# Keeping two Winograd partial sums in PSUM banks that ScalarE seeds and TensorE adds to, and holding back three products of a unit instead of two

## The chip, the cores and the metric

The kernel runs on one core of one Trainium2 chip. The metric is the device time of one execution in microseconds (us). Three runs of the kernel before gave 1256.2, 1257.9 and 1260.05 us, so its median is 1257.9 us.

## The reference, cut to what matters

One transformer layer on 2048 tokens of width 512, in fp32: an RWKV block (time mixing and channel mixing) and a gated feed-forward block, each behind a layer norm and added to its input.

```
h, hh = layer_norm(x), layer_norm(x) shifted by one token
k, v, r = three mixes of h and hh, each @ a 512x512 weight
x = x + (sigmoid(r) * wkv(k, v)) @ Wo.T
kk = mix(h, hh) @ Wkey.T            # 512 -> 2048
sr = sigmoid(mix(h, hh) @ Wcr.T)
x = x + sr * (silu(kk) @ Wval.T)    # 2048 -> 512
...
out = (silu(z @ gate.T) * (z @ up.T)) @ down.T      # 512 -> 2 x 2048 -> 512
```

Nearly all of the work is matrix products of 512 tokens with 512x512 blocks of weights.

## The kernel before, in words

**Tiling.** The tokens are worked in four blocks of 512 (`b` = 0 to 3). A product of a 512x512 activation block with a 512x512 weight block is not computed as eight products of 256x256 quarters but as seven, by Winograd's form of Strassen's scheme. One product of quarters is four calls of `nc.tensor.matmul` (two halves `m` of the output by two halves `k` of the contraction), and each call leaves two records in the trace, so a product is eight records of line 527 (4256 such records stand for 532 products). `plain_unit` (L619) does the first eight blocks of weights (k, r, v and out of token blocks 0 and 1) without the scheme; `unit` (L508) does everything else except the last down projection, which `down_product` (L1075) does with two levels of the scheme.

**One unit.** With quarters A of the weights and B of the activations, S and T their prepared sums and differences, the seven products are P1 = A11 B11, P2 = A12 B21, P3 = S4 B22, P4 = A22 T4, P5 = S1 T1, P6 = S2 T2, P7 = S3 T3. Their combination is a chain: with U2 = P1 + P6 and U4 = U2 + P5, the quarters of the result are P1 + P2 at (0, 0), U4 + P3 at (0, 1), U4 + P7 at (1, 1) and, with the signs of the prepared sums, U2 + P7 + P4 at (1, 0). In the code, one PSUM bank `z` collects P1, then P6, then P5, then P7 in place. On the way ScalarE copies it to SBUF three times (`snapshot`, L542 to L544): `s1` after P1, `u2` after P6, `u4` after P5. P2 goes to a bank `v` and P3 to a bank `x` of their own, and VectorE adds them to the copies (`add`, L546; `tt`, L362 and L363). P4 goes onto what `z` holds after P7, and VectorE adds the difference `u2` - `u4` to take the surplus out again. Each finished quarter goes to a `sink(i, j, c)` that the caller gives: two Relus and two exponentials on ScalarE for k (L830 to L841), a Tanh for r and the gate, a Silu for up and the feed-forward gate, VectorE multiplications or additions for v, out, up of the feed-forward and down.

**The order within a unit** is written out by hand: `order = (step1, step2, None, step3, step4, None, step5)` (L604). At each `None` one step held back from the unit before is run (`pop_held`, L502); steps 6 and 7 are appended to `held` for the unit after (L614). So a step that writes `z` again is always two products behind the copy that it has to wait for. A unit over four weight blocks (`down_unit`, L938, one for each token block) takes four products per step, one for each weight block; its order is (step1, step4, step3, step2, step5) (L607), and its step 1 pops held steps between its products (`between`, L539). The last of them (`loose`, token block 3) runs its held steps at once.

**What is mixed in.** Every engine runs its instructions in the order in which this Python program emits them. After every product `tick` (L287) lets background work be emitted: norms, transposes on TensorE (L414), the mixes (`mix`, L455: ScalarE writes `shifted`, L464, VectorE adds `mixed`, L472), sums of operands (`sums_of`, L435), and the preparation of weight sums (`prepare`, L140, whose loads go through GpSimd's queue). The planner counts VectorE time (`cost`, L200) against 88% of 1.72 us per product (`STEP`, `SHARE`) and holds work back when it has run ahead. `later(fn, n)` (L203) puts VectorE work off by n products, `due` (L281) emits it, and `flush` (L209) emits all of it. `Lazy` (L660) forces the operand sums of a unit out when they are first asked for.

**Buffers.** `ps` (L80) is one pool of eight PSUM banks for products and transposes. In the compiled kernel before, banks are handed out again in the order in which they came free. `up` has six SBUF tiles for the copies. The start runs `WARM` = 44 transposes of an identity into a bank (L332 to L334), then the norm, transposes (L769), mixes and the first product of `first_block` (L729).

**The units of the scheme, in order.** gate of block 0; four up units; down of block 0; k, r, v of block 2; gate of block 1; out of block 2; ups, down of block 1; k, r, v of block 3; gate, out, ups, down of block 2; gate, ups, down of block 3; then for each block of the feed-forward four gate and four up units (the first gate unit of the next block is put ahead) and the two-level down product.

Of the kernel before, what the change touches and what calls it, by code (L numbers as in the profile page):

```python
# [9 lines left out]
F32 = mybir.dt.float32  # L10
AF = mybir.ActivationFunctionType
ALU = mybir.AluOpType
# [3 lines left out]
P = 128  # L16
# [4 lines left out]
HB = TB // 2  # L21
# [3 lines left out]
STEP = 1.72  # L25
# [20 lines left out]

A11, A12, A22, A21, S1, S2, S3, S4 = range(8)
B11, B12, B21, B22, T1, T2, T4 = range(7)  # L50
T3 = B12
# [7 lines left out]
def rwkv_ffn_kernel(  # L59
# [8 lines left out]
    nc = tc.nc  # L68
# [8 lines left out]
    opp = ctx.enter_context(tc.tile_pool(name="opp", bufs=3))  # L77
    up = ctx.enter_context(tc.tile_pool(name="up", bufs=6))
    small = ctx.enter_context(tc.tile_pool(name="small", bufs=3))
    ps = ctx.enter_context(tc.tile_pool(name="ps", bufs=8, space=bass.MemoryType.PSUM))  # L80
    dram = ctx.enter_context(tc.tile_pool(name="dram", bufs=1, space=bass.MemoryType.DRAM))


# [8 lines left out]
    def u_tile(name):  # L92
        return up.tile([P, 2, HB], F32, tag="u", name=name)
# [14 lines left out]
    def flat(t):  # L108
        return t.rearrange("p a b -> p (a b)")
# [22 lines left out]
    def raw_quarters(n, eng):  # L132
        raw = []
        for k in range(4):
            t = wring.tile([P, 2, HB], F32, tag="w", name="w")
            eng.dma_start(t, w[n, k])
            raw.append(t)
        return raw
# [61 lines left out]
    def cost(n, fixed=0.135, per=0.00107):  # L200
        spent[0] += max(0.17, fixed + per * n)

    def later(fn, ticks=1):  # L203
        put_off.append([ticks - 1, fn])
# [8 lines left out]
    def step(item, wait):  # L213

        try:
            r = next(item[1])
        except StopIteration:
            item[4].remove(item)
            finished.add(item[2])
            return True  # L220
        return True if wait or r is None else None

    def run_one(wait):


        blocked = False
        for item in list(hot)[:1] + list(background)[:3]:
            ready = item[0]
            if ready is not None and not item[3]:
                if blocked or not ready():  # L230
                    blocked = True
                    continue
                item[3] = True
            if step(item, wait):
                return True
        assert not wait
        return False
# [7 lines left out]
    def prep_one():  # L245
        item = preps[0]
        if item[1] > 0:
            return False
        try:
            if next(item[2]) is not None:  # L250
                item[1] = WAIT
        except StopIteration:
            preps.popleft()
            finished.add(("sums", item[0]))
            if len(preps) > 1 and item[3] > 1:
                begin(preps[1])
            elif preps:
                begin(preps[0])
        return True
# [27 lines left out]
    def tick(length=STEP):  # L287
        for item in preps:
            item[1] -= 1
        slack[0] = max(min(slack[0] + SHARE * length - spent[0], 2.5), -2.5)  # L290
        spent[0] = 0.0
        credit[0] = min(credit[0] + credit[1], 2.0)
        while slack[0] > 0 and (hot or background or preps):
            go = False
            if preps and credit[0] >= 1 and prep_one():
                credit[0] -= 1
                go = True
            elif hot or background:
                go = run_one(False)
            slack[0] -= spent[0]  # L300
            spent[0] = 0.0
            if not go:
                break
# [18 lines left out]
    first = {WK: raw_quarters(WK, nc.sync)}  # L322
    first[WR] = raw_quarters(WR, nc.scalar)
    first[WV] = raw_quarters(WV, nc.sync)
    ident = const.tile([P, P], F32, name="ident")
# [7 lines left out]
    for _ in range(WARM):  # L333
        nc.tensor.transpose(pt[:, 0, 0:P], ident, ident)  # L334

    onem = const.tile([P, 5, NC], F32, name="onem")

    nfirst = const.tile([P, NC], F32, name="nfirst")
# [17 lines left out]
    def size(ap):  # L356
        n = 1
        for d in ap.shape[1:]:
            n *= d
        return n  # L360

    def tt(out, a, b, op):  # L362
        nc.vector.tensor_tensor(out, a, b, op)  # L363
        cost(size(out))
# [131 lines left out]
    held = []  # L496
# [5 lines left out]
    def pop_held():  # L502
        if held:
            length, step = held.pop(0)
            step()
            tick(length)

    def unit(weights, Bs, sink, by_token, done=None, free=None, loose=False):  # L508

        acc, tmp = {}, {}
        last = len(weights) - 1

        def product(z, a, b, first, between=None):
            if first:
                acc[z] = bank()
            pz = acc[z]
            wt = [weight(n, a) for n in weights]
            for g, wg in enumerate(wt):  # L520
                act = Bs[g][b]
                for m in range(2):
                    for k in range(2):
                        lo = slice(m * P, (m + 1) * P)
                        lhsT = act[:, k, lo] if by_token else wg[:, k, lo]
                        rhs = wg[:, k, :] if by_token else act[:, k, :]
                        mm = nc.tensor.matmul(  # L527
                            pz[:, m, :],
                            lhsT=lhsT,
                            rhs=rhs,  # L530
                            start=first and g == 0 and m == 0 and k == 0,
                            stop=g == last and k == 1,
                            skip_group_check=True,
                        )
                latest[:] = [mm.ins.name]
                due()
                if g < last:
                    tick()
                    if between is not None and g > 0:  # L539
                        between()  # L540

        def snapshot(name):  # L542
            tmp[name] = u_tile(name)
            nc.scalar.copy(tmp[name], acc["z"])  # L544

        def add(z, name):  # L546
            tt(tmp[name], acc[z], tmp[name], ALU.add)

        def step1():
            product("z", A11, B11, True, pop_held)  # L550
            snapshot("s1")

        def step2():
            product("v", A12, B21, True)
            add("v", "s1")
            sink(0, 0, tmp["s1"])

        def step3():
            product("z", S2, T2, False)
            snapshot("u2")  # L560

        def step4():
            product("x", S4, B22, True)

        def step5():
            product("z", S1, T1, False)
            snapshot("u4")

            def rest():
                add("x", "u4b")  # L570
                sink(0, 1, tmp["u4b"])

            def both():
                tt(tmp["u2"], tmp["u2"], tmp["u4"], ALU.subtract)
                if loose:
                    tmp["u4c"] = u_tile("u4c")
                    nc.vector.tensor_copy(tmp["u4c"], tmp["u4"])
                    cost(2 * HB)
                tmp["u4b"] = tmp["u4"]
                rest()  # L580

            later(both, 1)

        def step6():
            if loose:
                product("y", S3, T3, True)
                add("y", "u4c")
                sink(1, 1, tmp["u4c"])
                return
            product("z", S3, T3, False)  # L590
            sink(1, 1, acc["z"])

        def step7():
            if loose:
                tt(tmp["u2"], tmp["u2"], tmp["u4c"], ALU.add)
            product("z", A22, T4, loose)
            add("z", "u2")
            sink(1, 0, tmp["u2"])
            if free is not None:
                free()  # L600
            if done is not None:
                later(done, 2)

        order = (step1, step2, None, step3, step4, None, step5)  # L604
        if last > 0:

            order = (step1, step4, step3, step2, step5)  # L607
        for s in order:
            if s is None:
                pop_held()  # L610
            else:
                s()
                tick()
        held.extend(((STEP, step6), (STEP, step7)))  # L614
        if loose:
            release()
            flush()
# [457 lines left out]
    def down_product(b, sink, final):  # L1075
# [107 lines left out]
        for n in range(7):  # L1183
            t = DOWN[n][1]
            while (b, t if t != T3 else "T3") not in made:
                flush_one()
            one = steps(n)
            one[0]()
            tick(half)
            pop_held()  # L1190
            one[1]()
            tick(half)
            pop_held()
            for k in range(2, 5):
                one[k]()
                tick(half)
            held.extend((half, k) for k in one[5:])

    def ffn_down(b):
# [172 lines left out]
```

## Time and profile before

| | |
|---|---|
| median of three runs | 1257.9 us |
| the profiled execution, its own time | 1260.03 us |
| its span, first to last instruction | 1258.2 us |
| busy: TensorE matmul (PE), its weight loads (PEld) | 1240.0 us, 1110.7 us |
| busy: VectorE (DVE), ScalarE (ACT), GpSimd (POOL) | 777.4 us, 369.0 us, 151.3 us |
| granted TensorE clock | 0.997 |

Busy time is a union of records; the ends of matmuls are modelled, so a start-to-start distance is the safer measure of TensorE's pace. In the tables of groups a row gives line, engine, operation, output and inputs by the program's names without buffer numbers, shapes and count, then busy us and the mean ns of one, then the engine's idle time before them and what ended it. In a table of waits a row gives who waited, for whom, and then us in total, times, and the longest.

### The profile page before, as it was taken

Reading aid. Unit: us, or ns where it says so; the run is one execution under the profiler, and the core shown is the slowest. Engines: PE = TensorE matmul, PEld = TensorE weight load, DVE = VectorE, ACT = ScalarE, POOL = GpSimd, SP = SyncE. Lnnn points to the kernel's source line nnn. Section 1 sums busy time; section 2 is a strip of 40 time slices with the busy share of each in tenths; the row PEclk is TensorE's granted clock in tenths of the full one; section 3 lists DMA queues with packets and bytes.
Section 4 is the critical chain, followed back from the end, with each engine's and each line's share of the span. In section 5 each row is a group of like instructions: output and inputs, shape, how many; then the busy total and the mean of one; then the engine's idle time right before and its main releaser. Section 6 shows DMA issues by size and latency. Waiting matters only on the chain.

```text
span 1258.2 us, 18321 instructions
## 1 busy us (share of the span) xinstructions
PE 1240.0 (99%) x6572; PEld 1110.7 (88%) x6572; DVE 777.4 (62%) x1416; ACT 369.0 (29%) x687; POOL 151.3 (12%) x276
## 2 busy tenths in 40 slices
PE   9999999999999999999999999999999999999998
PEld 8888888878888888888888888998899988998898
DVE  5756577567786576743473466565766566564476
ACT  6533252252533433302320222112221223112211
POOL 2222211211222212122220000000000000000000
PEclk9999999999999999999999999999999999999999
DMA  6666777887787777789875654795459854785575
GB/s 205 222 209 232 242 242 255 258 269 243 246 264 243 268 251 244 233 279 332 273 253 183 221 154 144 242 337 175 143 169 301 284 154 146 231 291 165 152 220 199
DMA packets 137960, 288.55 MB, mean 229 GB/s; under 512 B 17296, under 2 KB 18320, under 8 KB 136848
## 3 DMA queue, kind: packets, MB, share of 16 engines
q1 hardware_dynamic: 115424, 215.53, 54.9%
q0 software_dynamic: 21440, 70.27, 15.6%
q10 hardware_dynamic: 1008, 1.59, 0.3%
q8 instruction: 53, 0.87, 0.3%
q14 instruction: 35, 0.29, 0.1%
HBM read 245.39 MB, written 41.94 MB: 228 GB/s over the span
## 4 chain that ended last, share of the span: by engine, by line
PE 93%; ACT 3%; DVE 2%; DMA 1%; issue 1%; POOL 0%; DVEq 0%
PE ps L527 71%; PE ps L1126 14%; PE ps L640 6%; PE ps L414 2%; ACT mix L465 1%; DMA raw<-in_w 1%; DVE u L363 0%; DMA w<-in_w 0%; DVE mix L371 0%; DMA x<-in_x 0%; ACT r L835 0%; ACT e L840 0%; DVE e L371 0%; ACT x L701 0%; ACT mix L782 0%
## 5 line engine op out<-in xcount | busy, mean ns | idle before, releaser
L527 PE MATMUL ps<-zT,w 128*128 128x256 f32 x1792 | 391.4, 379 | 0.0
L527 PEld LDWEIGHTS ps<-zT,w 128*128 128x128 f32 x1792 | 338.7, 190 | 45.4
L527 PE MATMUL ps<-mix,w 128*128 128x256 f32 x1232 | 275.9, 383 | 6.0 <-ACT s L544 6.0
L527 PEld LDWEIGHTS ps<-mix,w 128*128 128x128 f32 x1232 | 235.8, 192 | 40.1 <-ACT s L544 7.6
L363 DVE TENSOR_TENSOR u<-ps,u 128x512 f32<-128x512 f32 x128 | 88.5, 692 | 149.2 <-PE ps L527 144.8
L544 ACT COPY u<-ps 128x512 f32<-128x512 f32 x128 | 74.8, 584 | 319.4 <-PE ps L527 319.4
L527 PE MATMUL ps<-w,s 128*128 128x256 f32 x512 | 114.3, 379 | 0.0
L527 PEld LDWEIGHTS ps<-w,s 128*128 128x128 f32 x512 | 97.0, 190 | 13.1
L1126 PE MATMUL ps<-w,hid 128*128 128x128 f32 x832 | 104.7, 275 | 0.4 <-ACT r L1138 0.4
L1126 PEld LDWEIGHTS ps<-w,hid 128*128 128x128 f32 x832 | 99.5, 192 | 1.1 <-ACT r L1138 0.5
L527 PE MATMUL ps<-w,t 128*128 128x256 f32 x432 | 96.5, 379 | 3.1 <-issue 1.8
L527 PEld LDWEIGHTS ps<-w,t 128*128 128x128 f32 x432 | 81.8, 190 | 14.8 <-issue 2.2
L1126 PE MATMUL ps<-w,quads 128*128 128x128 f32 x704 | 89.5, 276 | 0.4 <-ACT r L1138 0.4
L363 DVE TENSOR_TENSOR s<-ps,s 128x512 f32<-128x512 f32 x64 | 44.2, 690 | 69.0 <-PE ps L527 54.0
L1126 PEld LDWEIGHTS ps<-w,quads 128*128 128x128 f32 x704 | 84.3, 192 | 1.1 <-ACT r L1138 0.5
L640 PE MATMUL ps<-mix,w 128*128 128x256 f32 x384 | 83.8, 379 | 1.1 <-DVE mix L371 1.1
L640 PEld LDWEIGHTS ps<-mix,w 128*128 128x128 f32 x384 | 72.6, 190 | 11.1 <-DVE mix L371 1.5
L363 DVE TENSOR_TENSOR u<-u,u 128x512 f32<-128x512 f32 x64 | 44.0, 688 | 51.7 <-ACT u L544 51.7
L1138 ACT COPY r<-ps 128x128 f32<-128x128 f32 x112 | 29.6, 264 | 142.7 <-PE ps L1126 142.7
L363 DVE TENSOR_TENSOR raw<-raw 128x512 f32<-128x512 f32 x92 | 63.2, 687 | 12.0 <-DMA raw<-d 4.5
L1208 POOL DMA_DIRECT2D out<-resid x12 | 8.6, 717 | 469.9 <-DVE resid L363 469.9
L363 DVE TENSOR_TENSOR hid<-hid 128x512 f32<-128x512 f32 x84 | 56.6, 687 | 1.1
(127 smaller groups left out, 1179.4 us busy)
## 6 DMA issues: line engine op xcount, KB each, us to landing
w<-sum SPq DMA_DIRECT2D x304, 256.0 KB, 3.3
w<-in_w SPq DMA_DIRECT2D x256, 256.0 KB, 3.3
w<-dd SPq DMA_DIRECT2D x112, 256.0 KB, 3.5
raw<-in_w POOLq DMA_DIRECT2D x48, 256.0 KB, 4.9
sum<-raw POOLq DMA_DIRECT2D x48, 256.0 KB, 3.9
w<-d SPq DMA_DIRECT2D x48, 256.0 KB, 3.4
q<-in_w POOLq DMA_DIRECT2D x36, 256.0 KB, 6.0
sum<-q POOLq DMA_DIRECT2D x36, 256.0 KB, 3.5
```

The source lines that it names most:

```text
L363: nc.vector.tensor_tensor(out, a, b, op)
L414: nc.tensor.transpose(flat[:, t * P : (t + 1) * P], h[:, t, c * P : (c + 1) * P], ident)
L465: nc.scalar.activation(dst(c), hT[:, c, 0:TB].rearrange("p (j t) -> p j t", j=2), AF.Copy, scale=onem[:, row - MK, c : c + 1],)
L527: mm = nc.tensor.matmul(pz[:, m, :], lhsT=lhsT, rhs=rhs, start=first and g == 0 and m == 0 and k == 0, stop=g == last and k == 1, skip_gro ...
L544: nc.scalar.copy(tmp[name], acc["z"])
L640: mm = nc.tensor.matmul(acc[i, j][:, m, :], lhsT=act[:, k, lo] if by_token else wg[:, k, lo], rhs=wg[:, k, :] if by_token else act[:, k, : ...
L1126: mm = nc.tensor.matmul(dst, lhsT=x[k][:, g, :], rhs=wt[:, g, :], start=first and g == 0, stop=g == 3, skip_group_check=True,)
L1138: nc.scalar.copy(st["r"][:, m, n * P : (n + 1) * P], st["z"])
L1208: eng.dma_start(out_t[b][:, 2 * j : 2 * j + 2, i * HB : (i + 1) * HB], rs[b][:, 2 * j : 2 * j + 2, i * HB : (i + 1) * HB],)
```

## The change

Two PSUM banks are taken out of the pool for good: `accv` and `accx` (the pool `ps` goes from eight banks to six). At the start eight matmuls of the identity are written into them, four each. In every unit ScalarE now copies P1 from `z` to `accv` (not to SBUF), and TensorE adds P2 to it in that bank; the sink of quarter (0, 0) reads `accv`. After P5, ScalarE copies `z` to `accx`, TensorE later adds P3 there, and the sink of (0, 1) reads `accx`. The VectorE additions of P2 and P3 are gone. `u2` is still copied to SBUF, and VectorE's subtraction reads `accx` in place of the SBUF copy of `u4`. In the `loose` unit ScalarE makes a second copy of `z` to SBUF in place of one by VectorE.

The steps are renamed after the products they run, and the order becomes 1, (held), 2, 6, (held), 5, (held); products 7, 3 and 4 are held for the next unit. The unit over four weight blocks runs 1, 2, 6, 5, and its step 1 pops a held step after each of its first three products instead of after the second and third only. The first quarter of the two-level down product pops one more held step.

```
+    ps = ctx.enter_context(tc.tile_pool(name="ps", bufs=6, space=bass.MemoryType.PSUM))
+    pv = ctx.enter_context(tc.tile_pool(name="pv", bufs=1, space=bass.MemoryType.PSUM))
+    px = ctx.enter_context(tc.tile_pool(name="px", bufs=1, space=bass.MemoryType.PSUM))
...
+    accv = pv.tile([P, 2, HB], F32, name="accv")
+    accx = px.tile([P, 2, HB], F32, name="accx")
+    for t in (accv, accx):
+        for k in range(4):
+            nc.tensor.matmul(
+                flat(t)[:, k * P : (k + 1) * P],
+                lhsT=ident,
+                rhs=ident,
+                start=k == 0,
+                stop=True,
+                skip_group_check=True,
+            )
...
-                    if between is not None and g > 0:
+                    if between is not None:
                         between()
...
         def step1():
             product("z", A11, B11, True, pop_held)
-            snapshot("s1")
+            acc["v"], acc["x"] = accv, accx
+            nc.scalar.copy(accv, acc["z"])
 
         def step2():
-            product("v", A12, B21, True)
-            add("v", "s1")
-            sink(0, 0, tmp["s1"])
...
+            product("v", A12, B21)
+            sink(0, 0, accv)
+
+        def step6():
+            product("z", S2, T2)
+            tmp["u2"] = u_tile("u2")
+            nc.scalar.copy(tmp["u2"], acc["z"])
 
         def step5():
-            product("z", S1, T1, False)
-            snapshot("u4")
...
+            product("z", S1, T1)
+            nc.scalar.copy(accx, acc["z"])
+            if loose:
+                tmp["u4"] = u_tile("u4")
+                nc.scalar.copy(tmp["u4"], acc["z"])
+            later(lambda: tt(tmp["u2"], tmp["u2"], accx, ALU.subtract), 1)
...
+        def step3():
+            product("x", S4, B22)
+            sink(0, 1, accx)
...
-        order = (step1, step2, None, step3, step4, None, step5)
         if last > 0:
-
-            order = (step1, step4, step3, step2, step5)
+            order = (step1, step2, step6, step5)
+        else:
+            order = (step1, None, step2, step6, None, step5, None)
...
-        held.extend(((STEP, step6), (STEP, step7)))
+        held.extend(((STEP, step7), (STEP, step3), (STEP, step4)))
...
                 one[k]()
                 tick(half)
+                if n == 0:
+                    pop_held()
```

More of the change, by code (lines that the diff above doesn't have):

```diff
@@ L79, in rwkv_ffn_kernel @@
     small = ctx.enter_context(tc.tile_pool(name="small", bufs=3))
-    ps = ctx.enter_context(tc.tile_pool(name="ps", bufs=8, space=bass.MemoryType.PSUM))
+    ps = ctx.enter_context(tc.tile_pool(name="ps", bufs=6, space=bass.MemoryType.PSUM))
+    pv = ctx.enter_context(tc.tile_pool(name="pv", bufs=1, space=bass.MemoryType.PSUM))
+    px = ctx.enter_context(tc.tile_pool(name="px", bufs=1, space=bass.MemoryType.PSUM))
     dram = ctx.enter_context(tc.tile_pool(name="dram", bufs=1, space=bass.MemoryType.DRAM))
@@ L513, in unit, with product @@
         last = len(weights) - 1
-        def product(z, a, b, first, between=None):
+        def product(z, a, b, first=False, between=None):
             if first:
@@ L538, in product @@
                     tick()
-                    if between is not None and g > 0:
+                    if between is not None:
                         between()
[L542 to L547, printed above, removed]
         def step1():
             product("z", A11, B11, True, pop_held)
-            snapshot("s1")
+            acc["v"], acc["x"] = accv, accx
@@ L553, in step2 @@
+            nc.scalar.copy(accv, acc["z"])
         def step2():
-            product("v", A12, B21, True)
-            add("v", "s1")
-            sink(0, 0, tmp["s1"])
[L558 to L563, printed above, removed]
-        def step5():
-            product("z", S1, T1, False)
-            snapshot("u4")
[L569 to L582, printed above, removed]
@@ L584, in step6 @@
-        def step6():
+            product("v", A12, B21)
[4 more added lines that the diff above has]
+            nc.scalar.copy(tmp["u2"], acc["z"])
+        def step5():
+            product("z", S1, T1)
[4 more added lines that the diff above has]
+            later(lambda: tt(tmp["u2"], tmp["u2"], accx, ALU.subtract), 1)
@@ L585, in step6, with step7 @@
+        def step7():
             if loose:
                 product("y", S3, T3, True)
-                add("y", "u4c")
-                sink(1, 1, tmp["u4c"])
+                tt(tmp["u4"], acc["y"], tmp["u4"], ALU.add)
+                sink(1, 1, tmp["u4"])
                 return
-            product("z", S3, T3, False)
+            product("z", S3, T3)
             sink(1, 1, acc["z"])
-        def step7():
+        def step3():
+            product("x", S4, B22)
+            sink(0, 1, accx)
@@ L594, in step7, with step4 @@
+        def step4():
             if loose:
-                tt(tmp["u2"], tmp["u2"], tmp["u4c"], ALU.add)
+                tt(tmp["u2"], tmp["u2"], tmp["u4"], ALU.add)
             product("z", A22, T4, loose)
-            add("z", "u2")
+            tt(tmp["u2"], acc["z"], tmp["u2"], ALU.add)
             sink(1, 0, tmp["u2"])
```

## The prediction

> **What bounds the kernel now.** I read the page first: busy times, then the chain of work that ended last.
>
> ```profile
> PE 1240.0 (99%) x6572; PEld 1110.7 (88%) x6572; DVE 777.4 (62%) x1416; ACT 369.0 (29%) x687; POOL 151.3 (12%) x276
> ...
> PE 93%; ACT 3%; DVE 2%; DMA 1%; issue 1%; POOL 0%; DVEq 0%
> ```
>
> TensorE is busy all the time and the chain lies on it. The chain in order of time gives its pace: in the longest unbroken pieces (start, length, records)
>
> ```profile
> 157.18 56.98 PE ps L527 x264
> ```
>
> 56.98/264 = 0.216 us per record, so 1.73 us per product of eight records. All 532 products run at that pace except at a handful of places; there only can the change win. The table of waits of TensorE names them:
>
> ```profile
> PE ps L527 <- ACT s L544: 6.0, 3, 2.3
> PE ps L527 <- issue: 1.8, 1, 1.8
> ...
> PE ps L527 <- ACT sr L914: 1.2, 1, 1.2
> ...
> PE ps L1126 <- ACT r L1138: 0.7, 2, 0.4
> ```
>
> Measured from start to start of single records, against 0.216, line 527 loses 11.2 us in all: at 265.6 us (3.0 with its after-effects), 432.2 (1.9) and 510.5 (2.3) behind the copy after P1, at 294.0 (1.5) and 458.3 (2.1) before P6 of an out unit, and some 0.4 in crumbs. **11.2 us is the most that the change can win in the units.** The groups show the additions that it removes and the copies that it redirects:
>
> ```profile
> L363 DVE TENSOR_TENSOR u<-ps,u 128x512 f32<-128x512 f32 x128 | 88.5, 692 | 149.2 <-PE ps L527 144.8 <-PE ps L414 1.8
> ...
> L544 ACT COPY u<-ps 128x512 f32<-128x512 f32 x128 | 74.8, 584 | 319.4 <-PE ps L527 319.4
> ...
> L363 DVE TENSOR_TENSOR s<-ps,s 128x512 f32<-128x512 f32 x64 | 44.2, 690 | 69.0 <-PE ps L527 54.0 <-ACT s L544 14.9
> ```
>
> Idle time before all three is ended by TensorE: they wait for it, not it for them.
>
> **What the Trainium skill says.** "PSUM — Partial Sum Buffer", section "PSUM: the matmul accumulator": a write by ScalarE doesn't change the bits that make a matmul add or overwrite, so a seed has to land where a matmul has written before; that is the purpose of the eight identity matmuls. The same page, "Engine vs sequencer instructions": ScalarE's and VectorE's queues are strictly first in, first out, and matmuls run in program order. The trace agrees: at 512 us (below) a copy that is ready waits behind a Silu. "Perfetto Trace Analysis", "Optimizing Scalar/DVE Operations": access costs ScalarE about 93 ns on SBUF and 51 on PSUM. No row here shows a ScalarE write to PSUM; by that page the copy would take 0.54 instead of 0.58 us, an estimate.
>
> **The change, part by part.**
>
> *Additions removed.* Two per unit of 64 units: 128 x 0.69 = 88 us of VectorE, 777 to 689. VectorE isn't on the path, so this gives nothing by itself; it can only shorten the waits listed above.
>
> *A copy that TensorE waits for at once.* What does it cost? The end of the program shows it, where a product into the same bank follows its copy directly:
>
> ```profile
> 1250.80 0.27 ACT L1138 COPY r<-ps 128x128 f32<-128x128 f32 x1 [1.52 <-PE ps L1126]
> ...
> 1251.12 1.16 PE L1126 MATMUL ps<-w,hid 128*128 128x128 f32 x8 [0.35 <-ACT r L1138]
> ```
>
> The last record before starts at 1250.49, so the distance is 0.63 where 0.11 is the pace: 0.52 lost for a copy of 0.27. For the copies of line 544: where ScalarE is free they start 0.42 to 0.47 us after the start of the product's last record (196.51 to 196.98), take 0.58, and TensorE starts 0.04 later: 1.04 - 0.22 = 0.82, and the first record after such a wait stands 0.32 from the second instead of 0.22, so **0.93 us**. Bounds: 0.89 with the cheaper write, 1.1 if ScalarE is held up a little.
>
> *Where that happens.* P2 may start only when P1's copy is in its bank, and P5 may write `z` only when `u2` is copied. In a single unit a held product (1.73 us) lies between, which hides 0.93. In the unit over four weight blocks the new order 1, 2, 6, 5 puts them back to back: before, 4, 3, 2 lay between. That is 2 in each of 4 down units: 8. Where nothing is held the `None`s are empty: the gate unit of block 0 is the first of its kind, and the first feed-forward gate unit follows the unit that has run its held steps at once: 2 + 2. Twelve x 0.93 = **+11.2 us**. Background work can't fill them but by luck: only transposes run on TensorE, 44 groups in the whole program. Against the down units' copies before: all 12 found ScalarE free (0.42 to 0.64), so the price isn't likely to be much above. Behind the waiting matmul stands all of TensorE's work, so each such wait moves the end. SP issues the weight loads in the new order of products; the page has them landing 3.3 us after issue, and the ring holds twelve of them (20 us of products), so that move costs nothing.
>
> *Eight identity matmuls at the start.* Each call leaves two records of 0.11 in fp32: 16 x 0.11 = 1.8 us behind the warm-up.
>
> ```profile
> 7.63 1.00 DVE L367 TENSOR_SCALAR h<-x,mv,two 128x512 f32<-128x512 f32 x2 [0.34 <-POOL two L749]
> ...
> 8.24 1.44 PE L769 MATMUL ps<-ident,h 128*128 128x128 f32 x8
> ...
> 9.06 0.56 ACT L774 ACTIVATE hT_a<-ps,vec 128x256 f32<-128x256 f32 x1 [5.40 <-DMA w<-in_w]
> ...
> 10.74 5.45 PE L640 MATMUL ps<-mix,w 128*128 128x256 f32 x24 [1.06 <-DVE mix L371]
> ```
>
> The warm-up ends at 8.23, and the first transposes follow; the second, which ScalarE at 9.06 needs, start at 8.69 when `h` is there. With 1.8 more they start at 10.1, and the whole chain to 10.74 moves: **+1.4 us** (0 if the scheduler finds another place, 1.8 at most).
>
> *Operand sums for the out units.* At 294 us TensorE waits for T2, which VectorE ends at 295.5 behind the addition and the sink of P2; the table puts this down to an activation that came last before.
>
> ```profile
> 294.45 0.60 ACT L914 ACTIVATE sr<-ps 128x512 f32<-128x512 f32 x1 [1.82 <-PE ps L527]
> ...
> 294.85 1.42 DVE L363 TENSOR_TENSOR t<-e,t 128x512 f32<-128x512 f32 x2
> ```
>
> After, the v unit's last product stands at the end of the gate unit, three products (5.2 us) before P6. VectorE then needs 0.42 + 4 x 0.69 = 3.2 us for P4's addition, its sink, T1 and T2. Two additions flushed at the unit's start and one after P2 are gone, so the planner has room to emit T1 and T2 in time. I take both waits as gone: **-3.6 us** (+2 if a weight sum gets in between).
>
> *The convoys.* The other three waits are of one kind:
>
> ```profile
> 508.26 1.33 ACT L465 ACTIVATE mix<-hT_b,onem 128x512 f32<-128x512 f32 x2
> ...
> 509.01 1.41 DVE L371 SCALAR_TENSOR_TENSOR mix<-hT_b,vec,mix 128x512 f32<-128x512 f32 x2 [1.52 <-ACT mix L465]
> ...
> 511.06 0.69 DVE L363 TENSOR_TENSOR u<-ps,u 128x512 f32<-128x512 f32 x1
> 511.79 0.63 ACT L924 ACTIVATE s<-u 128x512 f32<-128x512 f32 x1 [2.20 <-DVE u L363]
> 512.33 0.57 ACT L544 COPY s<-ps 128x512 f32<-128x512 f32 x1
> ...
> 512.95 1.42 PE L527 MATMUL ps<-mix,w 128*128 128x256 f32 x5 [2.06 <-ACT s L544]
> ```
>
> Mixes fill ScalarE, VectorE waits for them, P3's addition stands behind that, ScalarE's sink behind the addition, the next copy behind the sink. After, only the sink of P4 waits for VectorE. But TensorE's slack behind a copy falls from two products to one. From the end of P4's product: 0.42 + 0.69 + 0.63 + 0.58 and three hops of 0.05 are 2.5 us, and P2 of the next unit starts at 3.6: 1.1 us of slack, where a set of four mixes takes 2.7. Behind k in the r unit the sink is 2.1 us instead of 0.63, and the slack is gone: at least 0.3 lost there, twice, before any mix. I take the three waits as unchanged in sum: **0**, between -7.6 (all gone) and +7 (a set of mixes in each of the two r units and in two up units, 1.8 each).
>
> *Banks.* Six in the pool instead of eight; a unit holds one instead of three. Given out in the order of release, the first unit's last two quarters get the banks of transposes that were read long before: 0. If they got the bank of that unit's second quarter, which ScalarE reads at 27 us, it would be some 8; nothing speaks for it. The sinks now read PSUM instead of SBUF: VectorE 692 against 688 ns, nothing.
>
> **The sum** against the profiled execution (span 1258.2, time 1260.0): +11.2 + 1.4 - 3.6 + 0 = +9.0, so a span of 1267.2 and a time of 1269.0. That execution lies 2.1 above the median; from the median, 1257.9 + 9.0 = **1267 us**.
>
> **Rivals.** (1) *The freed VectorE ends every old wait.* All of the convoys go too, because three of four sinks no longer wait for VectorE: 11.2 + 1.4 - 11.2 = +1.4, some 1259.5, with crumbs 1257 to 1262: not slower. For it: each of the five waits has a VectorE addition in its chain. Against: half the slack. It decides once 9 of the 11.2 us are won back. (2) *The convoys grow*: with slack of one product, k's long sinks and the mixes stop TensorE in both r units for 2 to 5 us more, and the T2 waits stay in part: +16, some 1275. For it: lags of the copy after P1 of 2.9 and 5.5 us at 250 and 262, 3.2 and 4.9 at 416 and 429, where 1.1 will be free. (3) *The exposed copies are covered after all* by transposes that fall there and a cheaper write: 4 us less, 1263.
>
> **Chances.** Forecast 0.55 (1263 to 1272), rival 1 0.15, rival 2 0.20, rival 3 0.10. A measurement tells about 0.3% (3.8 us) from no change. Slower by more than that: the forecast, rival 2, rival 3 mostly: 0.83. Within: rival 1 mostly, 0.14. Faster 0.03. Range 1260 to 1275: half of rival 1 and half of rival 2 are left out.
>
> **What would show it.** Each down unit with two waits of line 527 for a copy, 0.8 long; two each at some 117 and 690 us; 16 records after the warm-up and the first product at 12.2; no wait before P6 of the out units; VectorE near 690 us. The prediction is wrong if the down units run through, or if waits between 250 and 270 and between 416 and 436 change by more than 4 us together.

## The result, and the profile after

The changed kernel takes 1263.61 us (median of six runs, 1263.10 to 1264.56) against 1258.05 for the kernel before beside it (six runs, 1256.20 to 1261.97): ratio 1.004, 95% interval 1.0025 to 1.0055. It is **slower by 5.6 us**; +9.0 was forecast. Its profiled execution took 1263.5 us with a span of 1261.4. All ratios here leave out one slow execution, of experiment 9 (1435.5 us at a granted clock of 0.85).

The page after has the same rows as before, busy time first, then the chain:

```profile
PE 1239.8 (98%) x6588; PEld 1108.6 (88%) x6588; DVE 689.1 (55%) x1287; ACT 368.1 (29%) x688; POOL 151.7 (12%) x276
...
PE 91%; ACT 5%; DVE 2%; issue 1%; DMA 1%; POOL 0%; ACTq 0%; DVEq 0%; POOLq 0%
```

VectorE lost the 88 us that it was to lose, and TensorE got 16 records more. The chain's share on ScalarE went from 3% to 5%: TensorE waits for ScalarE more than it did. The table of TensorE's waits says for what (who, for whom | us in total, times, longest):

```profile
PE accv L543 <- ACT accv L561: 8.8, 11, 1.3
PE ps L543 <- ACT u L570: 3.7, 5, 0.9
```

Two kinds of wait are left in the units, both for a copy: before P2, for the copy of P1 into `accv`, and before P5, for the copy of `z` to `u2`. The waits "issue" and "ACT sr", which were those for T2, are gone. The groups (count | busy us, mean ns | idle before, and what ended it):

```profile
L561 ACT COPY accv<-ps 128x512 f32<-128x512 f32 x64 | 36.6, 571 | 134.6 <-PE ps L543 134.4
L570 ACT COPY u<-ps 128x512 f32<-128x512 f32 x64 | 37.4, 585 | 120.9 <-PE ps L543 120.9
```

A copy into PSUM takes 571 ns (the copies to `accx`, L574, as well), one into SBUF 585. A down unit in the order of time, at the seam of P1 and P2:

```profile
201.18 0.57 ACT L561 COPY accv<-ps 128x512 f32<-128x512 f32 x1 [0.30 <-PE ps L543]
...
201.80 1.56 PE L543 MATMUL accv<-w,s 128*128 128x256 f32 x6 [0.66 <-ACT accv L561]
```

The copy starts 0.41 us after the start of P1's last record (200.77), and P2 starts 0.04 us after the copy's end: 1.04 us from record to record instead of 0.22, and the next one 0.32 instead of 0.22. That is 0.93 lost, as the prediction had it.

Where the time went, from the distances between the starts of TensorE's records in the two profiles (an excess over 0.216 us is a loss; a wait and the slow records right behind it together):

| | before | after | change | forecast |
|---|---|---|---|---|
| product directly behind its copy | 0 | 10.6 (11 waits) | +10.6 | +11.2 |
| T2 before P6 of an out unit | 3.5 | 0 | -3.5 | -3.6 |
| behind mixes and sinks in ScalarE's queue | 10.4 | 6.5 | -3.9 | 0 |
| other places in line 527 (after: 543) | 0.8 | 0.3 | -0.5 | - |
| start, to the first product | 10.74 | 11.91 | +1.2 | +1.4 |
| two-level down product (line 1126) | 1.9 | 1.3 | -0.6 | - |
| sum (change of the span: +3.2) | | | +3.3 | +9.0 |

The medians are 5.6 apart and not 3.2, because the profiled execution of the kernel before is 2 us above its median and that of the changed kernel is at its median.

The row that was forecast wrongly hides something that I had overlooked in the kernel before. Some stretches of its span, each 3.41 us long (start:end, length, then busy us and records of TensorE, its weight loads, VectorE, ScalarE and GpSimd, then the granted TensorE clock, the DMA share and GB/s):

```profile
264.92:268.33 3.41, 1.10 (x6) 0.62 (x5) 2.68 (x5) 1.28 (x4) 2.05 (x4) 1.00 0.78 223
268.33:271.75 3.42, 3.42 (x8) 2.79 (x9) 3.35 (x7) 0.41 (x1) 0.12 (x1) 0.50 0.75 268
...
432.17:435.59 3.42, 1.75 (x8) 1.22 (x8) 2.66 (x5) 1.60 (x3) 0.00 (x0) 1.00 0.73 231
...
510.68:514.09 3.41, 1.35 (x6) 1.04 (x6) 2.21 (x4) 1.54 (x3) 0.00 (x0) 1.00 0.44 132
514.09:517.51 3.42, 3.42 (x9) 2.72 (x9) 3.35 (x7) 1.26 (x3) 1.09 (x2) 0.50 0.23 30
```

After its waits of 2.5 us (at 265.6) and 2.2 us (at 510.5) the clock was at half for 3.4 us: some eight records at twice their distance, 1.7 us lost each time on top of the wait. The second of these stretches begins only at 514.09, 1.1 us after TensorE had gone on. After the wait of 1.8 us at 432 the clock stayed at 1.00. I had read the doubled distances as missing records.

### The profile page after: what moved, and what is told of

Same layout as the page of the kernel before. It is cut to its first block, busy times and chain, and to the rows that moved or that the text cites. A ratio compares the mean times of both kernels' runs of the same rounds, so it can differ in the third digit from the quotient of the medians.

```text
span 1261.4 us, 18153 instructions
## 1 busy us (share of the span) xinstructions
PE 1239.8 (98%) x6588; PEld 1108.6 (88%) x6588; DVE 689.1 (55%) x1287; ACT 368.1 (29%) x688; POOL 151.7 (12%) x276
## 4 chain that ended last, share of the span: by engine, by line
PE 91%; ACT 5%; DVE 2%; issue 1%; DMA 1%; POOL 0%; ACTq 0%; DVEq 0%; POOLq 0%
PE ps L543 48%; PE ps L1126 14%; PE accv L543 11%; PE accx L543 10%; PE ps L640 6%; PE ps L430 1%; ACT mix L481 1%; DVE u L379 1%; PE warm L337 1%; DMA raw<-in_w 1%; ACT accv L561 1%; ACT r L835 1%; ACT x L701 0%; ACT e L840 0%; DVE mix L387 0%
## 5 line engine op out<-in xcount | busy, mean ns | idle before, releaser
L543 PE MATMUL ps<-zT,w 128*128 128x256 f32 x1280 | 289.5, 379 | 0.7 <-ACT u L570 0.7
L543 PEld LDWEIGHTS ps<-zT,w 128*128 128x128 f32 x1280 | 241.8, 190 | 33.2 <-ACT u L570 1.1
L543 PE MATMUL ps<-mix,w 128*128 128x256 f32 x880 | 201.2, 379 | 0.0
L543 PEld LDWEIGHTS ps<-mix,w 128*128 128x128 f32 x880 | 167.0, 190 | 22.6
L379 DVE TENSOR_TENSOR u<-u,accx 128x512 f32<-128x512 f32 x64 | 43.9, 686 | 116.8 <-ACT accx L574 116.7
L640 PE MATMUL ps<-mix,w 128*128 128x256 f32 x384 | 83.8, 379 | 1.1 <-DVE mix L387 1.1
L640 PEld LDWEIGHTS ps<-mix,w 128*128 128x128 f32 x384 | 72.6, 190 | 11.1 <-DVE mix L387 1.5
L379 DVE TENSOR_TENSOR u<-ps,u 128x512 f32<-128x512 f32 x65 | 44.8, 690 | 65.0 <-PE ps L543 65.0
L574 ACT COPY accx<-ps 128x512 f32<-128x512 f32 x64 | 36.5, 571 | 144.2 <-PE ps L543 144.1
L561 ACT COPY accv<-ps 128x512 f32<-128x512 f32 x64 | 36.6, 571 | 134.6 <-PE ps L543 134.4
L570 ACT COPY u<-ps 128x512 f32<-128x512 f32 x64 | 37.4, 585 | 120.9 <-PE ps L543 120.9
L543 PE MATMUL accv<-zT,w 128*128 128x256 f32 x256 | 60.7, 380 | 0.7 <-ACT accv L561 0.7
L543 PE MATMUL accx<-zT,w 128*128 128x256 f32 x256 | 60.5, 379 | 0.0
```

The costliest lines, as they stand in the source:

```text
L543: mm = nc.tensor.matmul(pz[:, m, :], lhsT=lhsT, rhs=rhs, start=first and g == 0 and m == 0 and k == 0, stop=g == last and k == 1, skip_gro ...
L561: nc.scalar.copy(accv, acc["z"])
L570: nc.scalar.copy(tmp["u2"], acc["z"])
L574: nc.scalar.copy(accx, acc["z"])
L640: mm = nc.tensor.matmul(acc[i, j][:, m, :], lhsT=act[:, k, lo] if by_token else wg[:, k, lo], rhs=wg[:, k, :] if by_token else act[:, k, : ...
```

## Experiments

Ten runs. The first three undo one part each.

**1. The down units with their old order and additions.**

```
+        own = last > 0
...
+                order = (own1, own3, own6, own2, own5)
```

The steps `own1` to `own7` have P2 and P3 in banks of their own, and VectorE adds them.

> The changed kernel, but the four down units (four weight blocks each) keep the order 1, 3, 6, 2, 5 with banks of their own for P2 and P3 and VectorE additions, as before the change. Theory: in the profile of the changed kernel seven waits of these units, directly behind a copy, cost 6.8 us (six of 0.93 and one of 1.19); all seven go and nothing takes their place: 1263.6 - 6.8 = 1256.8 us, and no TensorE gap over 0.2 us in the down units. Rival (the time is only moved: the additions bring waits for VectorE back, and the k units behind have one step less to mix in): at least half of it returns in the k and r units, 1260 us or more.

Measured: 1255.54 us, ratio to before 0.9978 (0.9969 to 0.9987), 8.1 less than the changed kernel. All seven waits are gone:

```profile
PE accv L543 <- ACT accv L561: 5.0, 6, 1.3
PE ps L543 <- ACT u L570: 1.4, 2, 0.7
```

Eleven waits for `accv` became six and five for `u2` two. Nothing came back in the k and r units (1.56 at 266 and 429, as in the changed kernel); beyond the 6.8 us another wait of 1.4 us (at 509) went; why is not shown. With the copies of the down units exposed (no other product behind them) the kernel is slower than the one before; with the old order in these four units it is faster.

**2. The two units that find nothing held back, with the old order.** The same switch, for `last == 0 and not held`.

> The changed kernel, but the two units that find nothing held back (gate of token block 0, first feed-forward gate) keep the old order and VectorE additions. Theory: the four waits at 116.5, 120.9, 687.8 and 692.2 us of the changed kernel's profile (0.93, 0.98, 0.93, 0.94) go: 3.8 us less, 1259.8 us. Rival (TensorE is held by something else at these places too, such as operands that come late): less than 2 us, 1261.6 or more.

Measured: 1260.03 us, ratio 1.001 (1.0002 to 1.0017): 3.6 less, against 3.8 expected. The four waits are gone.

**3. A shorter warm-up.**

```
-WARM = 44
+WARM = 28
```

> The changed kernel with 28 instead of 44 warm-up transposes, so that the sixteen records of the identity matmuls lie inside the time of the warm-up. Theory: the first product of the program starts at 10.7 us again instead of 11.9, and the whole program is 1.2 us shorter: 1262.4 us. Rival (the startup is set by a transfer or by the norm that has its own time): no change, 1263.6, with the first product still at 11.5 or later.

Measured: 1262.65 us, ratio 1.0036 (1.0024 to 1.0049), 1.0 less than the changed kernel. The first product starts at 10.72, 1.2 earlier. In the profiled execution nine records at the start of the first product then ran at half pace (1.8 us lost), so that its span was 0.5 longer, not shorter. In this trace the clock is at half from 10.98 to 14.40 us, although no wait in front is longer than the one of 1.3 us before the first product, which the kernel before has too, there with a clock of 1.00. The four executions without the profiled one have a mean clock of 0.999 or 1.000 and took 1262.2 to 1262.8 us. So the shorter warm-up returns 0.8 to 1.4 us where the clock doesn't fall at the start.

**4. The kernel before once more.**

> The kernel before, unchanged, for a second profile of it. Its profiled execution was 2 us above its median, and in that profile TensorE ran at half its pace for some 3 us after each of its two longest waits (2.5 and 2.2 us). Theory: those half-pace stretches and the waits in front of them are what differs between executions; a second profile has the other gaps of line 527 unchanged to 0.2 us, and a shorter span goes with shorter waits or fewer half-pace records. Rival: the spread lies elsewhere (start, end, DMA), and line 527 loses the same 14.8 us again.

Measured: 1260.04 us under the profile, line 527 loses 14.8 us again at the same places to 0.1 us, half pace included. So the profile of before is reproducible, and with the same time twice it doesn't say what differs in the executions of 1256 us: inconclusive between theory and rival. The granted clock of the other executions says more; it is taken up in the next section.

**5. More slack behind P1.**

```
-            order = (step1, None, step2, step6, None, step5, None)
+            order = (step1, None, None, step2, step6, None, step5)
```

> The changed kernel with the order 1, held, held, 2, 6, held, 5 in single units: two products instead of one between the copy of P1 and P2, and the sink of P4 one product earlier. Theory: the waits of line 543 for the copy to accv at 167, 268, 332, 344, 433 and 509 us (6.5 us together) come from a ScalarE queue that is late by less than one more product (1.7 us), so all go: 1263.6 - 6.5 = 1257 us; the waits of the down units and of the two units with nothing held stay. Rival (the queue's delay only moves to the copies that have lost slack, after P5 and in the next unit): waits of the same sum elsewhere, 1262 or more.

Measured: 1271.65 us, ratio 1.0104 (1.0086 to 1.0122): 8 us **slower** than the changed kernel. The theory fell:

```profile
PE ps L543 <- ACT u L570: 6.8, 11, 0.9
PE accv L543 <- ACT accv L561: 4.2, 6, 0.7
PE accx L543 <- DVE u L379: 3.3, 3, 1.3
PE ps L543 <- ACT accx L574: 2.8, 2, 1.5
```

The waits for `accv` behind mixes are gone (six are left, the exposed ones), but P7 of the next unit now waits for the copy of `z` to `accx`, P3 for VectorE's subtraction, which has to read `accx` first, and three feed-forward units find only two short held steps and leave P6 and P5 without one between. The rival held. A seeded bank ties three engines to one place; a held product more behind one copy is one less behind another.

**6. The additions put back, the new order kept.** The changed order with P2 and P3 in banks of their own and VectorE's additions; down units as in experiment 1.

```
+        def late3():
+            product("x", S4, B22, True)
+            add("x", "u4")
+            sink(0, 1, tmp["u4"])
...
+            order = (own1, None, own2, own6, None, own5, None)
+            held.extend(((STEP, own7), (STEP, late3), (STEP, own4)))
```

> The order of the changed kernel (products 7, 3 and 4 held back) with the arithmetic of the kernel before: P2 and P3 in banks of their own, added by VectorE to SBUF copies; down units as in the kernel before. To be read against the run with the old down units (1255.5 us), from which it differs in the additions and in two fewer exposed copies (-1.9). Theory: the additions in the queue were what made the old waits, so with them back the waits for T2 before P6 of the out units return (some 3.5 us) and those behind mixes grow by some 4: about 1261 us. Rival (the new order alone ended the T2 waits and shortened the others): 1255.5 - 1.9 = 1253.6 us, no T2 wait.

Measured: 1255.07 us, ratio 0.9969 (0.9957 to 0.9982). No T2 wait, and the waits behind mixes sum to 5.6. **The theory fell and the rival held**: taking the additions away was not what ended the old waits, the order was. The trace of this run around the out unit of block 2 (start, us, what) shows how:

```profile
288.25 0.69 DVE L379 TENSOR_TENSOR u<-ps,u 128x512 f32<-128x512 f32 x1 [0.19 <-PE ps L543]
...
289.58 0.68 DVE L379 TENSOR_TENSOR t<-e 128x512 f32<-128x512 f32 x1
...
290.30 1.42 DVE L379 TENSOR_TENSOR t<-e,t 128x512 f32<-128x512 f32 x2
...
293.50 0.69 DVE L379 TENSOR_TENSOR s<-ps,s 128x512 f32<-128x512 f32 x1 [1.18 <-PE ps L543]
```

T1 and T2 (`t`) stand in VectorE's queue *ahead of* P2's addition (293.50). In the kernel before they stood behind it and its sink (`x`):

```profile
292.80 0.69 DVE L363 TENSOR_TENSOR s<-ps,s 128x512 f32<-128x512 f32 x1 [1.30 <-PE ps L527]
...
294.13 0.68 DVE L363 TENSOR_TENSOR t<-e 128x512 f32<-128x512 f32 x1
```

Two things in the code can have moved them: P3's addition is in a held step and no longer flushed at the out unit's start, and a held product stands between P1 and P2, in which the sums can be emitted. Experiment 10 tells more of this.

**7. As many VectorE additions as were removed, on a scratch tile.**

```
             product("v", A12, B21)
+            tt(spare, spare, spare, ALU.add)
             sink(0, 0, accv)
...
+            def both():
+                tt(tmp["u2"], tmp["u2"], accx, ALU.subtract)
+                tt(spare, spare, spare, ALU.add)
```

To make room for the scratch tile, the pool `up` has five tiles instead of six.

> The changed kernel with as many VectorE additions as it removed, on a scratch tile that nothing else reads, at the places in the queue where the old ones stood, and counted by the planner (VectorE near 777 us again). Nothing of the computation is left out. Theory: VectorE's load doesn't matter, only who waited for the additions: 1263.6 us within 1.5, no T2 wait, waits behind mixes as in the changed kernel to 1.5 us. Rival (the freed time is what ended the old waits, because the planner and the queue have room): T2 waits and longer waits behind mixes return, 1267 us or more.

Measured: 1263.0 us, ratio 1.0035 (1.0024 to 1.0046), VectorE busy 763 us. No T2 wait; behind mixes 6.1 us against 6.5. The theory held: VectorE's load is not what matters.

**8. A ladder of waits.** n additional copies by ScalarE ahead of the copy to `accv`, in seven units.

```
+                for _ in range(extra):
+                    nc.scalar.copy(more, acc["z"])
             nc.scalar.copy(accv, acc["z"])
```

> The changed kernel with 3, 4, 5, 6, 7, 8 and 9 additional ScalarE copies ahead of the copy to accv in seven feed-forward gate units, where TensorE otherwise never waits: waits of rising length, each 0.57 us longer than the last, from about 0.8 to 4.3 us (18 us in all). Theory: TensorE runs at half pace for 7 or 8 records (1.6 us more) after a wait of more than about 2.2 us and at full pace after one below 2.0, as in the profile of the kernel before after its waits of 2.5 and 2.2 and not after those of 1.8 and 2.0: four such stretches, about 1263.6 + 18 + 6.4 = 1288 us. Rival (the half pace in the kernel before came from something else than the wait's length): no half-pace records behind these waits, 1281.6 us.

Measured: 1291.06 us (two runs). From record to record, n = 3 to 9 made waits of 0.84, 1.46, 2.07, 2.69, 3.31, 3.92 and 4.54 us. After the first three the next records kept their pace; after each of the other four, seven to ten records ran at half pace (after the wait of 3.92 not at once, but from 0.9 us after it). Stretches of the ladder's trace with the third wait, and with and behind the fourth, columns as above:

```profile
997.04:1000.45 3.41, 1.89 (x9) 1.33 (x7) 0.69 (x1) 3.09 (x6) 0.00 (x0) 1.00 1.05 380
...
1024.34:1027.76 3.42, 0.93 (x5) 0.48 (x3) 2.42 (x6) 3.28 (x6) 0.00 (x0) 1.00 0.58 153
1027.76:1031.17 3.41, 3.37 (x8) 2.74 (x9) 1.94 (x6) 0.00 (x0) 0.00 (x0) 0.50 0.00 0
```

The theory held as far as it goes: the clock is 1.00 behind the wait of 2.07 and one half behind 2.69, so long waits of TensorE bring the half pace on. But the length is not all. All twelve traces have every change of the clock on a fixed grid: within a trace the changes lie whole multiples of 3.413 us apart, to 0.002 us (in the kernel before at 268.33, 271.75, 514.09 and 517.51), and the grid lies elsewhere against the program from trace to trace. Among the stretches of the grid that hold products of 256 columns alone, each of the nine in which TensorE was busy for 1.35 us or less was followed by a stretch at half clock, and none was in which it was busy for 1.57 us or more. So what a wait does depends on how much of it falls into one stretch: the wait of 2.0 us at 458 in the kernel before is cut by the grid at 459.48 (2.65 and 2.35 us busy) and left the clock at 1.00. In the changed kernel the longest wait is 1.5 us, no stretch from the first product to the last has less than 2.1 us, and the clock is 1.00 all the way.

**9. The order alone.** The kernel before, eight banks, no identity matmuls, VectorE's additions; only the order is the new one, and only in single units that find something held. The additional held steps that the change pops in the down units and in the two-level down product are kept.

```
+        three = last == 0 and bool(held)
...
+        elif three:
+            order = (step1, None, step2, step3, None, step5, None)
...
+            held.extend(((STEP, step6), (STEP, late4), (STEP, step7)))
```

Here `step3` runs P6, and the three held steps run P7, P3 and P4.

> The kernel before with nothing of the PSUM part: eight banks, no identity matmuls, VectorE additions. Only the order is the changed one (1, held, 2, 6, held, 5, held, with products 7, 3 and 4 held back), and only in single units that find something held; down units and the two units with nothing held keep the old order. Theory: what the change won lies in the order alone, and what it lost in the exposed copies and the identity matmuls; against the run with the additions back (1255.1 us) the two waits at 120 and 683 us (1.1 and 0.9) and 1.2 us at the start go: 1251.9 us, no T2 wait, waits behind mixes as in that run (5.4 us). Rival (the seeded banks also won something, by three sinks that don't wait for VectorE): 1254 us or more.

Measured: **1250.86 us**, ratio 0.9929 (0.991 to 0.9948). The theory held: no T2 wait; behind mixes 4.4 us:

```profile
PE ps L527 <- ACT s L544: 2.4, 2, 1.7
...
PE ps L527 <- ACT u L544: 0.9, 2, 0.5
```

**10. The same, with two products behind every copy.**

```
+            order = (step1, step2, None, step3, None, None, step5)
```

> As the run with the order alone, but 1, 2, held, 6, held, held, 5 in single units, so that two products lie behind every copy before z is written again (behind u2 there was one). Theory: the waits that are left (1.95 us twice at the k, r, v units, 0.6 to 0.9 twice) are waits for the copy to u2 or to s1 that is late by less than one more product: 3 us or more of the 5.4 go, 1249 us, and no TensorE wait is long enough for half pace. Rival (the delay only moves, as it did with two held products behind P1): within 1 us of the run with the order alone.

Measured: 1250.24 us, ratio 0.9929 (0.9912 to 0.9945): not to be told from experiment 9. Behind mixes 1.9 us are left instead of 4.4, but T2 is late again:

```profile
PE ps L527 <- ACT u L544: 1.4, 2, 0.9
...
PE ps L527 <- issue: 1.0, 2, 0.5
```

The line "issue" is the wait at 289 and 452 us (0.74 each from record to record): P2's addition and its sink (at 288.01 and 288.73) stand ahead of T2 (at 289.34) again. Of the 3 us or more that the theory promised behind mixes 2.5 were won, and 1.5 came back for T2, as the rival said. Both versions beat both kernels. P3's addition is in a held step here too; what differs from experiment 9 is that no held product stands between P1 and P2.

## Why the prediction was right or wrong

**Right: the price and the place of the exposed copies.** 0.93 us for a product behind its copy, in the down units and in the two units with nothing held, was measured within 0.02 where ScalarE was free (0.98 and 1.19 in two places where it wasn't); experiments 1 and 2 took the waits away and got 8.1 and 3.6 us back. Twelve were counted, eleven came: in the last down unit sixteen transposes fell between P6 and P5, the luck that the prediction named. The trace of the kernel before was enough, because its last two products showed a direct wait behind a shorter copy.

**Right: the start.** 1.2 against 1.4. The warm-up itself ended 0.2 us earlier. That the seeds need the identity matmuls, as the prediction takes from the Trainium skill, no run here shows: no kernel with seeded banks leaves them out.

**Right in size, wrong in its reason: T2.** Both waits went, -3.5 against -3.6. But I gave as reason that additions were removed; with the additions back (experiment 6) they stay away. What counts is that T1 and T2 stand ahead of P2's addition and its sink in VectorE's queue. The order brings this about: in experiments 6 and 9, with a held product between P1 and P2, they stand ahead; in experiment 10, without one, T2 stands behind and is late. That P3's addition is no longer flushed at the out unit's start is not enough, since that holds in experiment 10 too.

**Wrong: "I take the three waits as unchanged in sum: 0".** They fell by 3.9 us. 3.4 of these are the two stretches at half pace behind the waits of 2.5 and 2.2 us, which were in the trace and which I took for gaps in the records; so "11.2 us is the most that the change can win" should have read 14.8. The waits themselves, without those stretches, went from about 7 to 6.5, so as a forecast of the waits the 0 was nearly right. Its reason was not: the shorter chain that was to make up for the halved slack won nothing, for with VectorE's additions left in the new order has 5.6 and 4.4 us of these waits (experiments 6 and 9). The picture of the convoy was right: in the trace after, the wait at 268 us is k's sink and two mixes ahead of the copy, as described.

```profile
265.96 0.91 ACT L835 ACTIVATE r<-u,nfirst 128x256 f32<-128x256 f32 x2 [1.53 <-DVE u L379]
...
268.09 1.32 ACT L481 ACTIVATE mix<-hT_b,onem 128x512 f32<-128x512 f32 x2
...
269.32 0.58 ACT L561 COPY accv<-ps 128x512 f32<-128x512 f32 x1
...
269.95 1.99 PE L543 MATMUL accv<-mix,w 128*128 128x256 f32 x8 [1.30 <-ACT accv L561]
```

**Also left out:** the two-level down product gained 0.6 and the small gaps 0.5, for which the sum had no term. On the spans the sum is thus 5.8 us too high (+3.2 against +9.0). That the medians miss the forecast by only 3.4 us is luck: the median execution of the kernel before lost less to the clock than its profiled one. The rivals: number 1 (all old waits end) failed because waits of 6.5 us behind mixes are left; number 2 (they grow, and the T2 waits stay in part) failed because the T2 waits went and the others did not grow; number 3 happened once in twelve.

**The 2 us between the profiled executions of the kernel before and its median** go with the clock. The mean granted clock of every execution is on record. Of 59 executions of the kernel before beside the experiments, the 15 of 1256.0 to 1257.0 us had 0.999 or 1.000, the 22 of 1257.6 to 1258.8 us 0.998 or 0.999, the 15 of 1259.3 to 1260.9 us 0.997 but for one with 0.999, and the 7 of 1261.5 to 1262.9 us 0.996. The steps are of about the size of one stretch at half clock (1.7 us). In "TensorE: Matmul & The Clock Gate", section "What's actually happening", the Trainium skill says that the clock follows a free-running window of 3.4 us; the grid of 3.413 us in the traces agrees. By this the same wait would cost 1.7 us more in one execution than in another, by where the grid lies. All six executions of the changed kernel had 0.999 or 1.000: against executions of the kernel before with that clock (1256.4, the median of the 15) it is about 7.2 us slower, not 5.6.

**What stays open:** no execution of 1256 us has a trace, so that its waits are as long as the profiled ones and only lie otherwise on the grid is argued and not shown. Seeded banks with an order of the down units that keeps other work between copy and product were not run.

## What to carry to other kernels

A product that adds to a bank which ScalarE has just seeded, or that writes on in a bank which ScalarE is still copying, needs a product of other work in between; count the places where the order has none (units over several blocks, first units), for each costs the copy plus 0.35 us here, and the saved VectorE time didn't pay for it where VectorE wasn't the bound. When a change mixes a new order with new arithmetic, run the order alone: here the order alone took some 9 us off the kernel before (5.6 against its executions at full clock), and the changed kernel takes 12.8 us more than that. Experiments 1 to 3 took back 8.1, 3.6 and 1.0 of it one at a time, 12.7 in sum (they were not run together): what the seeded banks cost is the exposed copies and the start. Before you call a distance between matmuls a missing record, look at the granted clock of that stretch.

## What the runs showed of the hardware that I had not expected

- The granted clock changes only on a grid of 3.413 us (all twelve traces). A stretch of the grid with products of 256 columns in which TensorE was busy for 1.35 us or less was followed by one at 0.50 (seven to ten records, 1.6 to 2.3 us lost); one with 1.57 us or more was not. Where between the two the border lies, no run shows. With shorter matmuls in it the figures are others: in experiment 3 a stretch with 1.77 us busy, most of it transposes of 128 columns, was followed by half clock. Between products of 256 columns, waits up to 2.1 us left the clock at 1.00; those of 2.2, 2.5, 2.7 and more in these traces were followed by half clock.
- A ScalarE copy of 128x512 fp32 takes 571 ns into PSUM and 585 into SBUF (576 for the copies to `s1` in the kernel before): 5 to 14 ns less, where the Trainium skill's "Perfetto Trace Analysis" ("Optimizing Scalar/DVE Operations") let me expect some 42 (an estimate). Here the measurement decides.
